# Two attention layers on one core: layer 0's result transposed in 32x32 blocks on VectorE, other shared sums for q, k and v, narrowing copies and normalisations moved

## The chip, the cores and the metric

The kernel runs on one core of one Trainium2 chip. The metric is the device time of the whole kernel in microseconds (us), the median of several runs. Before the change it is 3349.99 us (three runs, 3349.24 to 3350.64).

## What is computed

There are 4096 nodes with 512 features and a 0/1 adjacency matrix. Layer 0 is a graph attention with 4 heads of 128, layer 1 a masked attention with 8 heads of 64. Both are added to their input and normalised over the features.

```python
# layer 0
support = (x @ weight).reshape(N, 4, 128).transpose(1, 0, 2)
logits = f1[:, None, :] + f2[:, :, None]      # f1, f2: support times weight_u, weight_v
w = where(logits >= 0, logits, 0.2 * logits)
attn = softmax(where(w * adj != 0, w * adj, -1e30)) * mask
x = layernorm(x + attn @ support + bias + x @ proj_w + proj_b)
# layer 1
q, k, v = (einsum('nd,hdk->hnk', x, W) for W in (Wqs, Wks, Wvs))
scores = q @ k.T * 64 ** -0.5 + 0.01 * eye - 1e16 * (1 - max(adj, eye))
x = layernorm(x + einsum('hqm,hmk,hko->qo', softmax(scores), v, Wo))
```

## The kernel before

The work is float32 on TensorE throughout, in three stages after a short start that ends at 216 us in the profile.

**Layer 0** (216 to 1136 us) goes over 4 quarters w of 1024 rows each, in each over 4 heads h (a quarter and head is a pass) and in each pass over 32 steps j, one for each 128 columns. In a step ScalarE makes the signs of the logits (`signs`, L625, two steps at once), VectorE masks them (`front`, L636, two steps at once) and makes the weights p (L641), and TensorE multiplies p with the values (L1076, 8 products, 16 records). The p tiles have four buffers, the z tiles of signs two. VectorE is written three steps ahead of TensorE (`LA = 3`). No scheduler reorders anything: each engine executes its instructions in the order in which the Python program issues them. `beside_unit(w, h, j)` issues, beside step u = 32 h + j of a quarter, the work for the next quarter, and `Later` runs a function a given number of steps later.

That work turns the adjacency into the form in which it is needed. A narrowing copy (`narrow`, L589) is a DMA on GpSimd's queue that reads a block of 1024 x 512 values in float32 and writes it as bf16 to DRAM; before it VectorE writes a token and GpSimd copies it, so that the copy starts when VectorE has come to that point. `turn_in0` (L595) transposes the block by DMA, on SP's queue, into one of two stage tiles. `shrink` (L601) is four ScalarE instructions that narrow it to fp8, and `keep` (L606) stores it for layer 1. A quarter has 8 such blocks c. SP's queue also carries, at the sixth step of each pass, the next pass's factors and values (3 MB, L616 and L987).

After the last head of a quarter `finish` divides (L1026), adds the projection by an accumulating DMA (L1040), and `close` takes the statistics of each of the quarter's eight row tiles (L511 and L513 on VectorE, L515 to L520 on GpSimd); `normalise` scales (L1049) and stores the tile to `x1_d`. `turn` then transposes the tile with four TensorE instructions (L1057), `turned` copies the result out of PSUM (L1062) and stores it to `x1T_d`, from which layer 1 reads it. In the last quarter the closing work runs on beside the first set of layer 1.

**q, k and v** (1137 to 1428 us) are made for 4 pairs of 512-row groups. For each pair there are three sets, k, q and v, and each is a product of 2x2 blocks done with seven block products instead of eight (`gemm`); `order` gives their order, `of_weights` and `of_features` the sums that they take as operands, and the plain ones take blocks as they are. A block product is 8 records of 0.43 us. Three of the seven accumulate in the PSUM tile of an earlier one. ScalarE, VectorE and GpSimd take the products out, combine and store them. The weights (`load_w`) are loaded with four DMAs each; wk in layer 0, wq and wv at the start of the stage. `beside` holds what is issued after a product. PSUM tiles come from `ps`, three buffers in the banks that layer 0's accumulators had, and from `xp`, two banks in which layer 0's transposes land.

**Attention of layer 1** (1428 to 3335 us): scores (L1127), exponential (L1341), mask (L1344), product with v (L1389), row sums on GpSimd and by accumulating DMAs (L1364, L1374), the output projection (L1453), and the closing normalisation.

## Time and profile before

| what | value |
|---|---|
| median of three runs | 3349.99 us |
| the profiled execution's own time | 3350.18 us |
| its span, first to last instruction | 3348.4 us |
| mean granted TensorE clock | 0.998 |
| TensorE busy | 3325.1 us (99%) |
| VectorE, ScalarE, GpSimd busy | 70%, 59%, 66% |
| TensorE transposes L1057 | 128 records, 19.2 us busy |
| ScalarE copies of them L1062 | 32, 18.5 us busy |
| ScalarE waiting for a transposed block (L601) | 9.5 us in 3 waits |

A row of the groups names line, engine, operation, output and inputs with their shapes, count, busy time and the mean of one in ns. A row of the waits says who waited for whom, for how long in total, how often and how long at most. A row of the timeline gives start and length in us, and in brackets the idle time before it and what ended it. TensorE's instructions overlap, so the sum of their lengths is more than the time that they take from one another; their starts tell that time.

### The profile page before, as it was taken

To read this page: it belongs to the slowest core of one execution; us is meant where nothing else is said; L and a number is where in the kernel's file an instruction comes from. 1 tells how busy PE (TensorE), PEld (TensorE's weight loads), DVE (VectorE), ACT (ScalarE), POOL (GpSimd) and SP (SyncE) were. 2 spreads that over 40 slices of the span, in tenths; PEclk is the share of its full clock that TensorE was granted. 3 is DMA by queue.
4 is the path that set the end of the run, shared out by engine and by line. 5 is a ranking of instruction groups with operands and counts; after the bars stand their busy time and mean duration, and the time that the engine had idled before them with its cause. 6 is when DMAs were issued, how large, how long until landed. Compare 5 with 4: busy or idle time off the path is not lost.

```text
span 3348.4 us, 66683 instructions
## 1 busy us (share of the span) xinstructions
PE 3325.1 (99%) x27096; PEld 1953.1 (58%) x27096; DVE 2359.6 (70%) x2894; ACT 1986.6 (59%) x2463; POOL 2218.8 (66%) x1588
## 2 busy tenths in 40 slices
PE   9999999999999999999999999999999999999998
PEld 8899999999999755643333333333333333333332
DVE  6689899898999611167776667676666666667676
ACT  1366977878776421256666656566565656656564
POOL 5631040040020365589999999999999999999996
PEclk9999999999999999999999999999999999999999
DMA  8988869589531443379899998889988889887984
GB/s 181 229 191 163 241 152 200 145 197 186 149 105 64 117 160 114 135 204 211 199 209 220 223 208 187 212 195 245 212 191 211 192 204 255 189 211 187 212 195 112
DMA packets 399054, 620.41 MB, mean 185 GB/s; under 512 B 166672, under 2 KB 247568, under 8 KB 397712
## 3 DMA queue, kind: packets, MB, share of 16 engines
q0 software_dynamic: 97520, 258.77, 42.5%
q1 hardware_dynamic: 299344, 354.26, 34.8%
q8 instruction: 215, 3.52, 0.4%
q10 hardware_dynamic: 1872, 3.02, 0.3%
q14 instruction: 103, 0.84, 0.1%
HBM read 315.87 MB, written 117.64 MB: 129 GB/s over the span
## 4 chain that ended last, share of the span: by engine, by line
PE 96%; POOL 1%; DVE 1%; issue 1%; DMA 1%; ACT 0%; SPq 0%; POOLq 0%; ACTq 0%; DVEq 0%
PE o_ps L1076 27%; PE o_ps L1389 26%; PE s_ps L1127 26%; PE s_ps L1192 5%; PE o_ps L847 4%; PE s_ps L1453 3%; PE s_ps L1185 3%; PE s_ps L1408 1%; PE x_ps L1057 0%; DMA p<-p 0%; DVE p L1521 0%; POOL q_sum L1364 0%; POOL s L700 0%; PE x_ps L1185 0%; DVE prod L818 0%
## 5 line engine op out<-in xcount | busy, mean ns | idle before, releaser
L1364 POOL TENSOR_TENSOR q_sum<-q_sum,p 128x1024 f32<-128x1024 f32 x538 | 1374.9, 2556 | 63.0 <-DMA p<-p 39.2
L1344 DVE TENSOR_TENSOR p<-s_ps,adjT 128x1024 f32<-128x1024 f32 x896 | 1043.8, 1216 | 465.3 <-ACT s_ps L1341 436.5
L1341 ACT ACTIVATE s_ps<-s_ps 128x1024 f32<-128x1024 f32 x1021 | 967.1, 1006 | 594.5 <-PE s_ps L1127 594.3
L1389 PE MATMUL o_ps<-p,v_sb 64*64 64x512 f32 x8192 | 943.6, 590 | 0.0
L1127 PE MATMUL s_ps<-q_sb,k_sb 64*64 64x512 f32 x8192 | 942.8, 589 | 0.2 <-DVE p L1344 0.2
L1076 PE MATMUL o_ps<-sup_t,p 128*128 128x129 f32 x8192 | 919.4, 275 | 1.2 <-DVE p L641 1.2
L1076 PEld LDWEIGHTS o_ps<-sup_t,p 128*128 128x128 f32 x8192 | 917.0, 192 | 1.6 <-DVE p L641 1.4
L641 DVE SCALAR_TENSOR_TENSOR p<-fr_t,dj,az 128x1024 f32<-128x1024 f32 x512 | 652.8, 1284 | 80.4 <-PE o_ps L1076 53.1
L1389 PEld LDWEIGHTS o_ps<-p,v_sb 64*64 64x64 f32 x8192 | 310.3, 133 | 570.6 <-issue 560.3
L1127 PEld LDWEIGHTS s_ps<-q_sb,k_sb 64*64 64x64 f32 x8192 | 312.8, 133 | 566.1 <-issue 456.1
L625 ACT ACTIVATE z<-fr_t,f 128x1024 fp8e4<-128x1024 f32 x512 | 558.0, 1144 | 119.4 <-DVE az L636 119.0
L1374 POOL DMA_DIRECT2D p<-p x412 | 437.2, 1297 | 10.2 <-PE o_ps L1389 8.5
L1040 POOL DMA_DIRECT2D agg<-base_d x32 | 28.7, 1206 | 516.0 <-ACT agg L1026 515.8
L1344 DVE TENSOR_TENSOR p<-s_ps,md 128x1024 f32<-128x1024 f32 x128 | 150.7, 1217 | 68.3 <-ACT s_ps L1341 63.6
L588 POOL COPY seen<-token 128x1 f32<-128x1 f32 x24 | 13.6, 565 | 252.9 <-DVE token L586 252.9
L636 DVE TENSOR_TENSOR az<-adjT,z 128x512 int32<-128x512 int32 x256 | 175.5, 686 | 2.1 <-ACT z L625 1.4
L1199 ACT ACTIVATE sb<-s_ps 128x1024 f32<-128x1024 f32 x35 | 35.8, 1024 | 192.6 <-PE s_ps L1192 129.8
L601 ACT ACTIVATE adjT<-stage 128x1024 fp8e4<-128x1024 bf16 x128 | 130.6, 1051 | 9.5 <-DMA stage<-adj_d 9.5
L1214 POOL TENSOR_TENSOR sb<-sb,sb 128x1024 f32<-128x1024 f32 x36 | 84.9, 2373 | 72.2 <-ACT sb L1199 72.2
L1238 DVE COPY k_sb<-s_ps 128x1024 f32<-128x1024 f32 x12 | 14.7, 1225 | 141.0 <-PE s_ps L1192 91.3
L1453 PE MATMUL s_ps<-wo_sb,on 128*128 128x512 f32 x240 | 110.8, 604 | 0.0
L1423 ACT ACTIVATE r<-r_h 32x256 f32<-32x256 f32 x248 | 102.3, 412 | 2.9
(179 smaller groups left out, 2139.4 us busy)
## 6 DMA issues: line engine op xcount, KB each, us to landing
p<-p POOLq DMA_DIRECT2D x412, 512.0 KB, 9.0
k_sb<-k_d SPq DMA_DIRECT2D x128, 512.0 KB
v_sb<-v_d SPq DMA_DIRECT2D x128, 512.0 KB
adj_d<-in_adj_dram POOLq DMA_DIRECT2D x32, 1024.0 KB, 10.9
sup_t<-sup_d SPq DMA_DIRECT2D x120, 258.0 KB
fr_t<-fr_d SPq DMA_DIRECT2D x16, 1024.0 KB
adjT_d<-adjT SPq DMA_DIRECT2D x32, 512.0 KB
adjT<-adjT_d SPq DMA_DIRECT2D x32, 512.0 KB
```

What stands on the lines that cost most here:

```text
L625: nc.scalar.activation(z[:, k, :], fr_t[w, h][:, 0, :], AF.Sign, bias=fs[j // GT][:, 0, (j + k) % GT, h:h + 1], saturate=False)
L636: nc.vector.tensor_tensor(az.bitcast(I32), adjT[w, j // CJ][:, j % CJ:j % CJ + 2, :].bitcast(I32), z.bitcast(I32), op=ALU.bitwise_and)
L641: nc.vector.scalar_tensor_tensor(p, fr[:, 1, :], dj[j // GT][:, j % GT, h:h + 1], az_t[w, h, j // 2][:, j % 2, :], op0=ALU.max, op1=ALU.mult)
L1076: nc.tensor.matmul(o[t // BK][:, t % BK, :], p[:, t * P:(t + 1) * P], s, start=(j == 0 and t % BK == 0), stop=(j == NT - 1), skip_group_ch ...
L1127: nc.tensor.matmul(s[c:c + MS, e, :], k[r, a + c:a + c + MS], qt[g, m][r, :], start=True, stop=True)
L1192: nc.tensor.matmul(half, a[:, c, n * P:(n + 1) * P], x[:, c, :], start=not more and c == 0, stop=c == 1, skip_group_check=True)
L1341: nc.scalar.activation(s, s, AF.Exp)
L1344: nc.vector.tensor_tensor(p, s, keep[:, None, :].to_broadcast([P, HP, G]), op=ALU.mult)
L1364: nc.gpsimd.tensor_tensor(q, q, p, op=ALU.add)
L1374: later.at(2, lambda: nc.gpsimd.dma_start(a, b, accum_op=ALU.add))
L1389: nc.tensor.matmul(o[c, n, :], v[r, j % CH, c], p[r, e, :], start=(j == 0), stop=(j == NT - 1))
L1453: nc.tensor.matmul(s, on_t[g][:, m, t * P:(t + 1) * P], wo_sb[:, m, :], start=(m == 0), stop=(m == NP1 - 1))
```

## The change

- The transposes of layer 0's result leave TensorE, with `turn`, `turned` and `x1T_d`. `x1_d` is kept by 512-row groups. `load_x1` reads half a group back in pieces of 32 rows by 128 features, and `turn_x1` transposes each 32x32 block on VectorE, into an order of the features that the weights follow (`load_w` loads 16 pieces per weight in that order). The first two groups are read and turned in the last quarter of layer 0, from step 72 on one transpose in three steps; the others in the k, q and v sets of the pair before.
- The seven products take other sums: sums are built on sums, and the results share one partial sum, u2. Feature sums of later pairs move from GpSimd to VectorE. The first product of the first set is of plain blocks and lands in `xp`. wv is loaded after the first set. The scaling of q moves from wq into the exponential.
- The narrowing copies of quarters 1 to 3: for quarter 1 one in 5 steps from step 16; for quarters 2 and 3 three at the end of the quarter before the usual one (steps 113, 118, 123), the other five from step 13. Transpositions start at step 50 or 48, one in 8 steps, and wait for a VectorE memset of two elements of the stage tile; `shrink` follows 8 steps after (14 before) and `keep` 15.
- The statistics of a quarter's tiles follow each other at 5/2 steps, from step 10 on (3/2 from step 12 before), except in the last quarter.

The diff, cut to its core:

```diff
-    order = (2, 3, 4, 5, 1, 6, 7)
...
+    order = (1, 5, 2, 6, 7, 3, 4)
+    of_weights = {5: ((1, 0), (1, 1), ALU.add), 6: (5, (0, 0), ALU.subtract),
+                  7: ((0, 0), (1, 0), ALU.subtract), 3: ((0, 1), 6, ALU.subtract)}
+    of_features = {5: ((0, 1), (0, 0), ALU.subtract), 6: ((1, 1), 5, ALU.subtract),
+                   7: ((1, 1), (0, 1), ALU.subtract), 4: ((1, 0), 6, ALU.subtract)}
+    plain_weights = {1: (0, 0), 2: (0, 1), 4: (1, 1), 7: (1, 0)}
+    plain_features = {1: (0, 0), 2: (1, 0), 3: (1, 1)}
...
             stage[w, c] = adjT_p.tile([P, CJ, W], BF16, name="stage", bufs=2)
+            if w:
+                nc.vector.memset(stage[w, c][:, 0, 0:2], 0.0)
             nc.sync.dma_start_transpose(stage[w, c], adj_d[w][c])
...
+        ys, xTs = {}, {}
+
+        def load_w(dst, src, c, a):
+            f = a * P + c * SQ
+            nc.sync.dma_start(dst[a * SQ:(a + 1) * SQ, c],
+                              src[:, f:f + SQ, :].rearrange("h p k -> p h k"))
+
+        def load_x1(g, n, pool=turn_p):
+
+
+
+            if n == 0:
+                xTs[g] = pool.tile([P, KC, G], F32, name="xT1", bufs=2)
+            ys[g, n] = turn_p.tile([P, HG // SQ, P], F32, name="y1_sb", bufs=2)
+            for a in range(NQ):
+                nc.sync.dma_start(
+                    ys[g, n][a * SQ:(a + 1) * SQ],
+                    x1_d[g][n * HG:(n + 1) * HG, a * P:(a + 1) * P].rearrange(
+                        "(b r) f -> r b f", r=SQ))
+
+        def turn_x1(g, n, c):
+            nc.vector.transpose(
+                xTs[g][:, c, n * HG:(n + 1) * HG].rearrange("p (b r) -> p b r", r=SQ),
+                ys[g, n][:, :, c * SQ:(c + 1) * SQ])
...
-                        first, step = (44, 9) if w else (52, 8)
-                        if u == (16 + 8 * c if w else 22 + 7 * c):
+                        first, step = (48, 8) if w else (50, 8)
+                        if u == (13 + 5 * (c - 3) if w else 16 + 5 * c) and c >= min(3, 3 * w):
                             narrow(w + 1, c)
+                        if c < 3 and w + 2 < NW and u == 113 + 5 * c:
+                            narrow(w + 2, c)
                         if u == first + step * c:
                             turn_in0(w + 1, c)
-                        if u == min(first + 20 + step * c, H0 * NT - 1):
+                        if u == first + 15 + step * c:
                             keep(w + 1, c)
                         if w == 0 and u == 98 + 3 * c:
                             keep(0, c)
                         for k in range(CJ):
-                            if u == first + 14 + step * c + 4 * k // 3:
+                            if u == first + 8 + step * c + 4 * k // 3:
                                 shrink(w + 1, c, k)
-                elif u % 4 == 0 and NT <= u < NT + 4 * KC:
-                    load_w(wk, wks, (u - NT) // 4)
-                elif u == NT + 4 * KC + 16:
+                elif NT <= u < NT + KC * NQ:
+                    load_w(wk, wks, (u - NT) // NQ, (u - NT) % NQ)
+                elif u == NT + KC * NQ + CJ:
                     nc.vector.tensor_tensor(wk_low, block(wk, 1, 0), block(wk, 1, 1), op=ALU.add)
-                elif h == H0 - 1 and j in (NT // 2, NT // 2 + CJ):
-                    load_xT((j - NT // 2) // CJ)
+                elif u >= 2 * NT and u % CJ == 0:
+                    k = (u - 2 * NT) // CJ
+                    if k % 3 == 0 and k < 12:
+                        load_x1(k // 6, k // 3 % 2)
+                if w + 1 == NW and u >= 2 * NT + 8 and (u - 2 * NT - 8) % 3 == 0:
+                    k = (u - 2 * NT - 8) // 3
+                    if k < 16:
+                        turn_x1(k // 8, k // 4 % 2, k % 4)
...
-                        later.at(12 + (3 * t // 2 if w + 1 < NW else 2 * t),
+                        later.at(10 + 5 * t // 2 if w + 1 < NW else 12 + 2 * t,
...
-                    nc.sync.dma_start(x1_d[i], y)
-                later.at(6, normalise)
-                later.at(8 if w + 1 < NW else 11, lambda: turn(y, i))
...
+                    nc.sync.dma_start(x1_d[i // GT][i % GT * P:(i % GT + 1) * P, :], y)
+                later.at(5 if w + 1 < NW else 6, normalise)
...
-            for dst, src in ((wq, wqs), (wv, wvs)):
+            def load_all(dst, src):
                 for c in range(KC):
-                    load_w(dst, src, c)
+                    for a in range(NQ):
+                        load_w(dst, src, c, a)
+
+            load_all(wq, wqs)
...
+            wk_s, wq_s = [spare()], [spare() for _ in range(2)]
+            wk_s = {5: wk_low, 6: wk_s[0][:, 0], 3: wk_s[0][:, 1], 7: block(wk, 1, 0)}
+            wq_s = {5: wq_s[0][:, 0], 6: wq_s[0][:, 1], 3: wq_s[1][:, 0], 7: block(wq, 1, 0)}
+            wv_s = {i: sp.tile([P, 2, D // 2], F32, name=f"wv_s{i}", bufs=1) for i in (5, 6, 3)}
+            wv_s[7] = block(wv, 1, 0)
...
+                a, c = (sums[k] if isinstance(k, int) else block(w, *k) for k in (a, c))
...
+                a, c = (x_s[k] if isinstance(k, int) else features(pair, *k) for k in (a, c))
...
-                sb = {i: sp.tile([P, 2 * G], F32, name=f"sb{i}", bufs=1) for i in (2, 3, 1)}
+                u2, p5 = (sp.tile([P, 2 * G], F32, name=n, bufs=2) for n in ("u2", "p5"))
...
                 for i in order:
-                    if i in (2, 3) or i == 6:
+                    if i == (7 if last else 1 if kind == "k" and pair == 0 else 0):
+                        t[i] = [xp.tile([P, GT, P], F32, name="x_ps").rearrange(
+                            "p t r -> p (t r)") for _ in range(2)]
+                    elif i in (1, 5, 6, 7):
                         t[i] = new()
-                    elif i == 1:
-                        t[i] = [xp.tile([P, GT, P], F32, name="x_ps").rearrange(
-                            "p t r -> p (t r)") for _ in range(2)] if last else new()
                     else:
-                        t[i] = t[{4: 2, 5: 3, 7: 1}[i]]
-                    if i == 7 and last:
+                        t[i] = t[{2: 1, 3: 5, 4: 7}[i]]
+                    if i == 4 and last:
                         for n in range(3):
                             first[n] = score(0, 0, n)
-                            nc.scalar.activation(first[n], first[n], AF.Exp)
-                    product(i, t[i], more=i in (4, 5, 7))
-                    if i in sb:
-                        copy(sb[i], t[i])
-                    if i == 3:
-                        pool(sb[3], sb[3], sb[2], ALU.subtract)
-                    elif i == 4:
+                            nc.scalar.activation(first[n], first[n], AF.Exp, scale=float(KD) ** -0.5)
+                    product(i, t[i], more=i in (2, 3, 4))
+                    if i == 1:
+                        copy(u2, t[i])
+                    elif i == 5:
+                        copy(p5, t[i])
+                    elif i == 2:
+                        copy(out["11"], t[i])
+                        store("11")
+                    elif i == 6:
+                        add(u2, t[i])
+                    elif i == 7:
+                        add(out["22"], t[i])
+                        pool(out["22"], out["22"], p5, ALU.add)
+                        later.at(1, lambda: store("22"))
+                    elif i == 3:
+                        add(out["12"], t[i])
+                        store("12")
+                    elif last:
                         copy(out["21"], t[i])
+                        pool(out["21"], out["21"], u2, ALU.add)
+                        store("21", nc.gpsimd)
+                    else:
+                        add(out["21"], t[i])
                         store("21")
...
                         fn()
                     later.step()
...
+                more = pair + 1 < NG // 2
+                halves = [(2 * pair + 2 + n // 2, n % 2) for n in range(4)] if more else []
+
+                def bring(n):
+                    load_x1(*halves[n], turn_p if pair % 2 else sp)
+
+                def turn(n):
+                    for c in range(KC):
+                        turn_x1(*halves[n], c)
+
                 beside = {}
...
+                    combine_features(nc.vector, 0, 5)
+                    for n, i in ((1, 6), (5, 7), (2, 3)):
+                        beside.setdefault(n, []).append(
+                            lambda i=i: combine_weights(nc.vector, wk, wk_s, i))
+                    for n, i in ((1, 6), (5, 7), (2, 4)):
+                        beside.setdefault(n, []).append(
+                            lambda i=i: combine_features(nc.vector, 0, i))
+                    for i, n in ((5, 7), (6, 7), (7, 3), (3, 4)):
                         beside.setdefault(n, []).append(
                             lambda i=i: combine_weights(nc.gpsimd, wq, wq_s, i))
+                if more:
+                    for k, n in ((5, 0), (7, 1)):
+                        beside.setdefault(k, []).append(lambda n=n: bring(n))
+                if pair == 0:
+                    beside.setdefault(4, []).append(lambda: load_all(wv, wvs))
                 gemm(wk, wk_s, "k", pair, beside)
                 beside = {}
                 if pair == 0:
...
+                    for i, n in ((5, 5), (6, 2), (7, 6), (3, 7)):
+                        beside.setdefault(n, []).append(
                             lambda i=i: combine_weights(nc.gpsimd, wv, wv_s, i))
-                if pair == NG // 2 - 1:
+                if more:
+                    for k, fn, n in ((1, turn, 0), (5, turn, 1), (5, bring, 2), (6, bring, 3),
+                                     (4, turn, 2)):
+                        beside.setdefault(k, []).append(lambda fn=fn, n=n: fn(n))
+                else:
...
-                if pair + 1 < NG // 2:
-                    for i in of_features:
-                        beside.setdefault(i, []).append(
-                            lambda i=i: combine_features(nc.gpsimd, pair + 1, i))
+                if more:
+                    beside[1] = [lambda: turn(3)]
+                    for i, n in ((5, 5), (6, 6), (7, 7), (4, 4)):
+                        beside.setdefault(n, []).append(
+                            lambda i=i: combine_features(nc.vector, pair + 1, i))
...
-                    nc.scalar.activation(s, s, AF.Exp)
+                    nc.scalar.activation(s, s, AF.Exp, scale=float(KD) ** -0.5)
```

## The prediction, made before the changed kernel was run

> **What bounds the kernel now.** I read first the page's busy times, then TensorE's waits, then TensorE in order of time at the places that the change touches, then what VectorE and the queues do beside it.
>
> ```profile
> PE 3325.1 (99%) x27096; PEld 1953.1 (58%) x27096; DVE 2359.6 (70%) x2894; ACT 1986.6 (59%) x2463; POOL 2218.8 (66%) x1588
> ```
>
> TensorE is busy 3325.1 of 3348.4 us, and its own list of waits is nearly empty. Of its longer rows these three touch the change:
>
> ```profile
> PE o_ps L1076 <- DVE p L641: 1.2, 1, 1.2
> PE s_ps L1192 <- ACT agg L1026: 1.1, 1, 1.1
> PE s_ps L1192 <- POOL adjT L1156: 0.7, 1, 0.7
> ```
>
> So from 216 us on the span is a sum of matmul work: time can be won by taking work off TensorE or by removing the last two waits, and by nothing else; it is lost wherever another engine makes TensorE wait. TensorE in order of time, at a normalisation and at the layer boundary (start, duration, count):
>
> ```profile
> 475.79 0.60 PE L1057 MATMUL x_ps<-ident,agg 128*128 128x128 f32 x4
> 476.23 3.74 PE L1076 MATMUL o_ps<-sup_t,p 128*128 128x129 f32 x32
> ...
> 1134.78 1.61 PE L1076 MATMUL o_ps<-sup_t,p 128*128 128x129 f32 x13
> 1137.50 3.70 PE L1192 MATMUL s_ps<-xT,wk_low 128*128 128x512 f32 x8 [1.10 <-ACT agg L1026]
> ```
>
> Four transposes show 0.60 us, but the next matmul starts 0.44 us after they do. The last product of layer 0 ends at 1136.39 and q, k, v begin 1.10 us later.
>
> What can make TensorE wait in layer 0 is VectorE's chain (timeline, one cycle of two steps) and the blocks of adjacency that DMA transposes (timeline of the SP queue and of ScalarE):
>
> ```profile
> 444.98 0.68 DVE L636 TENSOR_TENSOR az<-adjT,z 128x512 int32<-128x512 int32 x1
> 445.77 2.48 DVE L641 SCALAR_TENSOR_TENSOR p<-fr_t,dj,az 128x1024 f32<-128x1024 f32 x2
> 448.17 0.68 DVE L636 TENSOR_TENSOR az<-adjT,z 128x512 int32<-128x512 int32 x1
> ```
> ```profile
> 563.00 11.92 SPq L595 DMA_TRANSPOSE stage<-adj_d  x1
> ...
> 587.29 2.00 ACT L601 ACTIVATE adjT<-stage 128x1024 fp8e4<-128x1024 bf16 x2 [4.07 <-DMA stage<-adj_d]
> ```
>
> VectorE needs 448.17 - 444.98 = 3.19 us for two steps. TensorE needs 32 records: the chain has 1888 records in 210.84 us, 0.1117 each, so 3.57 us. VectorE has 0.19 us a step to spare. The transposed block issued at 563.00 was usable only at 587.29, 24.3 us later, with a narrowing copy in flight (that copy's row: 8.2/10.9/25.0 us to landing, minimum, median, maximum).
>
> **What the Trainium skill says.** "TensorE: Matmul & The Clock Gate", Part 4: PE-mode transpose, gives about 275 ns for a transpose in a kernel, mostly access latency. The trace agrees on the duration (273 ns mean, L1057), but in the stream one costs 0.109 us, so I price by spacing. "VectorE: DVE Perf Modes", The three transpose paths, says that VectorE transposes only 32x32 blocks, each in place in its grid: hence the change's loads in 32-row pieces and its permuted weight loads. Layer 0 of this trace does the same (L741). "DMA: Bandwidth & Descriptors", Issuing engines are not separate DMA queues, says that DMAs of all issuing engines interleave on the same 16 engines; the 24.3 us above agree.
>
> **The change, part by part.**
>
> *Transposes off TensorE.* Two groups of four and 48 records take 482.02 - 475.79 = 6.23 us; 48 x 0.1117 = 5.36; so a group costs 0.87 / 2 = 0.435 us. 32 groups x 0.435 = **13.9 us** off the path: 24 groups (10.4) in layer 0, 8 (3.5) in q, k, v. ScalarE's 32 copies (L1062, 587 ns, 18.5 us) and 32 SP stores go with them; neither is waited for.
>
> *In their place* 64 VectorE transposes 128x256, 413 ns each (L741). Sixteen fall in the last quarter of layer 0, one in three steps: 0.41 against 3 x 0.19 = 0.57 us to spare, so hidden; if there were no cover, 6.6 us. Each waits for its load; queued behind it on VectorE are the next p tiles, and TensorE behind those. The load is issued at least 8 steps (14 us) earlier, from rows written hundreds of us before, in a stretch where DMA is at 0.15 of its share (1000 to 1100); a similar strided load took 5.9 us at the start. So nothing. The other 48 (19.8 us) lie in q, k, v, where VectorE was busy 14.70 of 100 us (1200 to 1300). The loads are 4 SP issues per half in place of one per tile; weights take 16 issues instead of 4. wq is issued before the boundary and needed 24 us (one set of seven products) after it; 16 issues at the 0.72 us of today's larger ones are 11.6 us. wv is issued a set later and needed 48 us after the boundary. Nothing.
>
> *Shared sums.* Seven products a set before and after, three of them accumulating: TensorE's work is the same. A set's evictions go from 4 ScalarE copies, 3 VectorE and 4 GpSimd passes to 3, 4 and 1; the feature sums go from GpSimd (2.35 us) to VectorE (1.2 to 1.9). Each product lasts 3.44 us (8 x 0.43), the longest eviction 1.23, and a PSUM tile is needed again at the earliest one product later, so no wait appears. The first product now takes plain operands and a PSUM tile that nobody else holds: the 1.1 us wait goes; its next need, the first freed bank, is 3.44 us later, and the divisions that free the banks end at 1137.96, before 1136.4 + 3.4. The q set's first product no longer needs a GpSimd sum: **0.7 us** go. What is late next: the fifth product's feature sum, one 1.2 to 1.9 us VectorE instruction from 1136.7, in time. In the last set one thing turns against it: the second early score takes the tile that the product just before it used. That tile is free 1.23 us plus some 0.2 of signalling after the product; the first score covers 0.91 (2.74 for three). **+0.5 us.** wq's scaling (1.9 us on ScalarE) moves into the exponential's scale: nothing.
>
> *Normalisations.* A tile's statistics hold VectorE 0.82 us (458.89 to 459.71). Before, two tiles in three steps: 4.79 + 1.64 = 6.43 against TensorE's 6.23. After, two in five steps: 7.98 + 1.64 = 9.62 against 8.94, because TensorE no longer pauses: 0.68 lost per pair, 2.7 us over four pairs. VectorE's lead is three p buffers less its own instruction, 5.36 - 1.28 - 0.3 = 3.8 us. It holds, with 1.1 us left; without spreading it would not.
>
> *Narrowing copies and transposed blocks.* Three of eight copies go to the end of the quarter before, where DMA was at 0.14 (635 to 645); in quarters 1 and 2 the rest are issued by step 33 and the first transposition comes at 48, so those no longer meet. But a new two-element memset makes each transposition wait for VectorE, and ScalarE takes the block 8 steps (14.3 us) later in program order instead of 14. Behind the memset on VectorE stand the p tiles, but the buffer it waits for was given up 4 steps earlier: nothing. Behind the held transposition on SP stand stores and the next pass's loads, due many steps later. The price is on ScalarE: a block must land about 14.3 - 1.05 (narrowing to fp8) - 2.3 (two signs) = 11 us after the memset or VectorE waits, and some 4 us of VectorE's lead later, 15 us, or TensorE waits. Alone, a block kept DMA busy 0.60 + 0.14 of ten us (625 to 645), 7 us: in time. In quarter 0 all eight copies run at one per 5 steps (8.9 us) and the last overlap the first transposition (step 50 against 46 and 51). Bounds there: 0, if the queues share evenly and the block takes twice its 7 us; 24.3 - 15 = 9 us, if the old collision returns. No gain is possible, since TensorE has no such wait now. I take **+1.2 us**, nearer to zero because only 3 of 32 blocks were waited for (9.5 us in total).
>
> *Sum*, against the profiled execution's own 3350.18 us (span 3348.4 plus 1.8; 0.2 above the runs' median 3349.99, which I leave): 3350.2 - 13.9 - 1.1 - 0.7 + 0.5 + 1.2 = **3336.2 us**.
>
> **Rivals.**
> (a) *The old collision in quarter 0*: 9 us of stall instead of 1.2, 3344.0. For: the 24.3 us row, and copies closer together than before. Against: a lead on ScalarE and VectorE that hid the same lateness then.
> (b) *VectorE becomes layer 0's bound* and the 10.4 us won there are lost to p tiles: 3336.2 + 10.4 - 1.2 = 3345.4, within 0.2%. For: 9.62 against 8.94 in the normalisations. Against: VectorE waited 53.1 us for TensorE in layer 0 (L641's idle row).
> (c) *Slower*: every transposed block of the three quarters (24) lands late, since all now have 8 steps. The place is ScalarE's narrowing; the point is a landing more than 15 us after the memset. The net gain without stalls is 15.2; 0.2% (6.7 us, about what a measurement of this kernel can tell from no change) slower needs (15.2 + 6.7) / 24 = 0.9 us a block. At 2 us a block: 3350.2 - 15.2 + 48 = 3383. For: an SP issue of a transposition takes 6.5 us in the median and up to 15.9. Against: the uncrowded ones take 3.9 to 4.1 and most now run without a copy.
>
> **How the numbers follow.** Forecast 0.62 (3333.5 to 3340), (a) 0.16 (to 3344), (b) 0.13, (c) 0.09. Low end: no stall and no late score (-1.7) and 1.0 for the spread of runs (3349.24 to 3350.64) and rounding, 3333.5. High end: (a), 3344.0; the two hold about 0.8. Faster is below 3343.3: the forecast, (a), and a little of (b), 0.81; same 0.10; slower 0.09.
>
> **What would show it.** Right: no TensorE transposes; q, k, v starting within 0.1 us of layer 0's last product; layer 0 about 10 us shorter and q, k, v about 5; attention unchanged. Wrong: TensorE rows waiting for p (L641's successor) in layer 0, with ScalarE's narrowing waiting for the transposed block (a, c) or VectorE without waits (b); or TensorE waits inside the sets.

## The result, and the profile after

The changed kernel takes 3332.69 us (median of five runs, 3330.72 to 3333.58). The kernel before, timed beside it, took 3350.07 us (3349.24 to 3351.37). The ratio is 0.9946, with a 95% interval of 0.9932 to 0.9961. The forecast was 3336.2 us, and the result lies 0.8 us below its low end of 3333.5. The direction and the main mechanism were forecast; the gain came out larger than the range allowed.

The profiled execution is the longest of the five, 3333.58 us (span 3331.7). I cut both profiles at four marks of TensorE: the first product of layer 0 (`o_ps<-sup_t,p`), the first product of q, k, v, the first score, and the last tiny matmul at the end.

| stage (us) | before | after | difference | forecast |
|---|---|---|---|---|
| start, to layer 0's first product | 209.23 | 209.12 | -0.1 | 0 |
| layer 0 and the boundary | 928.27 | 916.78 | -11.5 | -10.4 - 1.1 + 1.2 |
| q, k, v to the first score | 290.21 | 285.60 | -4.6 | -3.5 - 0.7 + 0.5 |
| attention | 1907.57 | 1908.53 | +1.0 | 0 |
| tail | 13.12 | 11.67 | -1.45 | 0 |

The busy times of the page after answer to the first fence of the prediction. TensorE has 128 matmuls fewer (27096 to 26968) and is still at 99%; VectorE took on work, GpSimd gave some up:

```profile
PE 3310.5 (99%) x26968; PEld 1938.6 (58%) x26968; DVE 2403.4 (72%) x3005; ACT 1955.9 (59%) x2419; POOL 2106.7 (63%) x1535
```

TensorE's list of waits (us in total, times, longest) begins so after the change:

```profile
PE o_ps L846 <- ACT z L863: 3.0, 1, 3.0
PE o_ps L886 <- POOL ident masks.py:199: 1.4, 1, 1.4
PE o_ps L1087 <- DVE p L640: 1.2, 1, 1.2
PE s_ps L1578 <- DVE all_ok L537: 1.0, 1, 1.0
```

The rows for `ACT agg` (1.1) and `POOL adjT` (0.7) are gone. The `DVE p` row is the same single wait of 1.2 us at layer 0's start that the kernel before has; no further wait for p has come. TensorE in order of time at the layer boundary shows the two effects there:

```profile
1099.77 26.29 PE L1087 MATMUL o_ps<-sup_t,p 128*128 128x129 f32 x234
1125.90 3.60 PE L1208 MATMUL x_ps<-xT,wk 128*128 128x512 f32 x8
1129.33 3.60 PE L1208 MATMUL s_ps<-adjT,wk_low 128*128 128x512 f32 x8
```

The group of layer 0 runs to 1126.06 by its modelled end, and q, k, v start at 1125.90 with no bracket, so with no wait. The next product comes 3.43 us later. In layer 0 the engines that prepare p wait like this (ScalarE's and VectorE's rows of waits):

```profile
ACT adjT L600 <- DMA stage<-adj_d: 17.8, 13, 2.7
```
```profile
DVE p L640 <- PE o_ps L1087: 38.9, 131, 0.3
...
DVE az L635 <- ACT z L624: 0.7, 1, 0.7
```

ScalarE now waits for a transposed block 13 times where it did 3 times, but never longer than 2.7 us (4.1 us before). VectorE lost nothing new by that: its one wait of 0.7 us for ScalarE lies at 238.9 us, and the kernel before has it too, at 239.0. VectorE still waited 38.9 us for TensorE, so TensorE remains the bound.

### The profile page after: what moved, and what is told of

Same layout as the page of the kernel before. It is cut to its first block, busy times and chain, and to the rows that moved or that the text cites. A ratio compares the mean times of both kernels' runs of the same rounds, so it can differ in the third digit from the quotient of the medians.

```text
span 3331.7 us, 66521 instructions
## 1 busy us (share of the span) xinstructions
PE 3310.5 (99%) x26968; PEld 1938.6 (58%) x26968; DVE 2403.4 (72%) x3005; ACT 1955.9 (59%) x2419; POOL 2106.7 (63%) x1535
## 4 chain that ended last, share of the span: by engine, by line
PE 95%; POOL 2%; DMA 1%; DVE 1%; issue 1%; ACT 0%; SPq 0%; POOLq 0%; DVEq 0%
PE o_ps L1087 27%; PE o_ps L1424 26%; PE s_ps L1138 25%; PE s_ps L1208 6%; PE o_ps L846 4%; PE s_ps L1488 3%; PE s_ps L1201 3%; DMA p<-p 1%; PE s_ps L1443 1%; POOL q_sum L1399 0%; DMA y_sb<-in_x_dram 0%; DVE p L1556 0%; POOL s L699 0%; PE x_ps L1201 0%; PE x_ps L1208 0%
## 5 line engine op out<-in xcount | busy, mean ns | idle before, releaser
L640 DVE SCALAR_TENSOR_TENSOR p<-fr_t,dj,az 128x1024 f32<-128x1024 f32 x512 | 650.4, 1284 | 67.1 <-PE o_ps L1087 38.9
L1230 POOL TENSOR_TENSOR k_sb<-k_sb,p 128x1024 f32<-128x1024 f32 x12 | 30.7, 2560 | 192.1 <-DVE k_sb L1236 187.8
L1215 ACT ACTIVATE u<-s_ps 128x1024 f32<-128x1024 f32 x11 | 11.3, 1024 | 173.4 <-PE s_ps L1208 110.1
L1236 DVE TENSOR_TENSOR u<-s_ps,u 128x1024 f32<-128x1024 f32 x12 | 14.7, 1225 | 106.2 <-PE s_ps L1208 76.3
```

Source lines behind the costliest of these rows:

```text
L640: nc.vector.scalar_tensor_tensor(p, fr[:, 1, :], dj[j // GT][:, j % GT, h:h + 1], az_t[w, h, j // 2][:, j % 2, :], op0=ALU.max, op1=ALU.mult)
```

## The experiments

Each kernel was timed in five rounds beside the kernel before, whose medians lay at 3350.7 to 3352.6 us. "Layer 0" and "q, k, v" are the stages of the table above, from each kernel's profile.

| kernel | median us | ratio to before, 95% interval | layer 0 | q, k, v |
|---|---|---|---|---|
| again_changed, the changed kernel | 3334.43 | 0.9956 (0.9943 to 0.9969) | 916.76 | 285.60 |
| e1 transposes back | 3346.66 | 0.9985 (0.9979 to 0.9992) | 927.00 | 289.11 |
| e2 old sums | 3336.22 | 0.9959 (0.9947 to 0.9972) | 918.03 | 286.70 |
| e3 old narrowing | 3369.99 | 1.0067 (1.0049 to 1.0085) | 937.44 | 285.61 |
| e4 no spread | 3339.24 | 0.9967 (0.9955 to 0.9978) | 922.13 | 285.61 |
| e5 fp8 copies after 4 steps | 3413.42 | 1.0187 (1.0173 to 1.0200) | 993.10 | 285.60 |
| e6 old narrowing and pauses | 3374.09 | 1.0057 (1.0038 to 1.0076) | 954.20 | 289.12 |
| e7 before with new narrowing | 3349.59 | 0.9998 (0.9990 to 1.0007) | 928.34 | 290.21 |
| e8 stores back | 3352.61 | 1.0003 (0.9995 to 1.0011) | 949.30 | 289.12 |
| e9 addresses back | 3369.67 | 1.0065 (1.0046 to 1.0085) | 944.83 | 289.12 |
| e10 first product in ps | 3334.64 | 0.9950 (0.9938 to 0.9963) | 918.03 | 285.70 |
| e11 no memset | 3338.21 | 0.9961 (0.9948 to 0.9974) | 918.55 | 285.61 |
| e12 old narrowing, memset | 3341.98 | 0.9967 (0.9955 to 0.9980) | 927.06 | 285.60 |
| e13 fp8 copies after 6 steps | 3336.43 | 0.9951 (0.9937 to 0.9964) | 919.66 | 285.60 |

A stage is read from one profiled run, and where runs scatter that run need not be typical: e3's (3357.9 us) and e11's (3333.6 us) were the shortest of their runs, e8's (3371.0 us) the longest. For kernels whose runs scatter (e3, e6, e9) the ratio differs a little from that of the medians. The first four shared one set of runs of the kernel before, e4 to e7 the next, e8 to e11 the third, e12 and e13 the last. again_changed repeats the changed kernel:

> The changed kernel once more, unchanged. Theory: the profile repeats layer 0 (910.1 us from the first wait to q, k, v) and q, k, v (285.6) to 0.2 us; the spread between runs of some 3 us comes from the attention stage and the end. Rival: layer 0 varies by 1 us or more.

It gave 3334.43 us (3333.13 to 3340.59). Layer 0 and q, k, v repeat to 0.02 us between the two profiles; what differs lies in the start, attention and the tail. The longest run, 3340.59 us, was not the profiled one.

**e1: the transposes.** Four TensorE transposes per row tile are put back; nothing reads them.

```
+                later.at(7 if w + 1 < NW else 11, lambda: turn_again(y))
+            def turn_again(y):
+                p = xp.tile([P, KC, P], F32, name="x_ps")
+                for c in range(KC):
+                    nc.tensor.transpose(p[:, c, :], y[:, c * P:(c + 1) * P], ident)
```

> The changed kernel with four TensorE transposes per row tile put back where they stood (two steps after the normalisation, eleven steps after the statistics in the last quarter); nothing reads their result, and the new path by VectorE stays. Theory (the gain is TensorE's own time): 32 groups x 0.435 us = 13.9 us more than the changed kernel, about 3346.6 us, 10.4 of it in layer 0 and 3.5 in q, k, v. Rival (the gain came from the freed ScalarE copies, stores and the new schedule): less than 7 us more, under 3340.

Measured: +12.2 us in the median over again_changed, +12.8 in the profile's span. Layer 0 grew by 10.2 us for 24 groups and q, k, v by 3.5 for 8, which is 0.43 a group in both. The spacing of the instructions was the right price.

**e2: the sums.** The products, sums and evictions of the kernel before, with the new transposes and schedule. With them come the old place of wv's load and the scaling of q in wq.

> The changed kernel with the sums, the order of the seven products and the evictions of the kernel before; transposes by VectorE, loads and schedule of layer 0 as changed. Theory (TensorE's work is the same, only two waits differ): the waits of 1.1 us at the boundary and 0.7 us at the first q set come back, with some 0.1 us each for filling TensorE again: 2.0 us more than the changed kernel, about 3334.7. Rival (the lighter evictions shorten q, k, v as such): the whole 4.6 us by which that stage became shorter beyond layer 0, less the 3.5 us of transposes, is smaller than 2, so to part them the profile must show waits inside the sets; 4 us or more would speak for it.

Measured: +1.8 us in the median. TensorE's list of waits has both rows again:

```profile
PE s_ps L1206 <- ACT agg L1051: 1.1, 1, 1.1
...
PE s_ps L1206 <- POOL adjT L1170: 0.7, 1, 0.7
```

Layer 0 with the boundary is 1.3 us longer and q, k, v 1.1, so each wait costs 0.2 to 0.4 more than its row. Most of this can be seen in the order of time. The row counts from the modelled end of the last record, but without a wait the next product starts 0.16 us ahead of that end (1125.90 against 1126.06 above); and a product that starts after a wait is followed by the next 3.54 us later, not 3.43.

The two experiments together account for both stages: 10.2 + 1.3 = 11.5 us in layer 0 and 3.5 + 1.1 = 4.6 us in q, k, v. So the moved narrowing copies and normalisations won no time of their own; the experiments below show what they prevent.

**e10: the bank of the first product.** One condition is changed.

```
-                    if i == (7 if last else 1 if kind == "k" and pair == 0 else 0):
+                    if i == (7 if last else 0):
```

> The changed kernel with the first product of the first k set in a bank of layer 0's pool again instead of one that nobody else holds. Theory: the 1.1 us wait of TensorE for ScalarE's last divisions returns at the start of q, k, v, with that row in the list of waits, and nothing else: +1.1 us. Rival (the plain operands alone removed it): no wait, within 0.3 us of the changed kernel.

In this kernel's list of waits the row of the boundary is back, in full:

```profile
PE s_ps L1208 <- ACT agg L1049: 1.1, 1, 1.1
```

Layer 0 is 1.3 us longer than in the changed kernel. Plain operands alone would not have removed this wait; the free bank did. The median, 0.2 us over again_changed's from another set of runs, is too coarse to show 1.1 us.

**e4: the spreading of the normalisations.**

```
-                        later.at(10 + 5 * t // 2 if w + 1 < NW else 12 + 2 * t,
+                        later.at(12 + (3 * t // 2 if w + 1 < NW else 2 * t),
...
-                later.at(5 if w + 1 < NW else 6, normalise)
+                later.at(6, normalise)
```

> The changed kernel with the closings and normalisations of a tile spaced as before (two row tiles in three steps instead of five, normalisation a step later); all else as changed. By the prediction VectorE needs two tiles' statistics in three steps: 4.79 + 1.64 = 6.43 us against 5.36 us of TensorE without its pauses, 1.07 us lost per pair, 4.3 us over the four pairs of a quarter, against a lead of 3.8 us. The prediction's step (without spreading it would not hold): TensorE waits for p of about 0.5 us in each of the first three quarters, 1.5 us in all, +1.5 us. Rival (the lead is larger than reckoned, or regained between the pairs): no row of TensorE waiting for p in the middle of layer 0 and the time of the changed kernel within 0.5 us; VectorE's idle time there merely shrinks.

The row of TensorE's waits for p in this kernel:

```profile
PE o_ps L1087 <- DVE p L640: 5.0, 7, 1.2
```

One of the seven is the 1.2 us of every kernel; 3.8 us are new, and layer 0 is 5.4 us longer. The step holds in kind (without spreading, VectorE's lead is used up). I had reckoned 1.5 us in all, so the lead was overrun by more than the 0.5 us a quarter of my sum. The 1.6 us of layer 0 beyond the six waits are again some 0.3 us for each.

**e13 and e5: how late a block may be.** ScalarE takes a block 6 or 4 steps after its transposition instead of 8. e5 has this edit, e13 has a 6 in the same place:

```
-                            if u == first + 8 + step * c + 4 * k // 3:
+                            if u == first + 4 + step * c + 4 * k // 3:
```

> The changed kernel with ScalarE taking a transposed block 6 steps (10.7 us) after the transposition instead of 8. By the prediction's reckoning VectorE waits for blocks that land later than 7.4 us after the memset and TensorE for those later than 11.4 us. The changed kernel's own longest wait of ScalarE for a block was 2.7 us at 8 steps; at 6 steps it would be 6.3 us, at most 2 us more than VectorE's lead. Theory: TensorE waits at a few blocks, under 5 us in all, 3333 to 3340 us. Rival (as with 4 steps, where TensorE's waits came to 55 us, the lead is used up at every block): 20 us or more over the changed kernel.

> The changed kernel with ScalarE taking a transposed block 4 steps (7.15 us) after the transposition was issued instead of 8 (14.3 us). By the prediction's reckoning a block must then land 7.15 - 1.05 - 2.3 = 3.8 us after the memset or VectorE waits, and within about 7.8 us or TensorE waits. The changed kernel's first block was usable after 9.0 us. Theory: VectorE waits for ScalarE at nearly each of the 24 blocks, TensorE for p at the slower ones, about 1 us each, +5 to +30 us, all of it in layer 0; a small result would say that the blocks land sooner than the waits of the changed kernel let one see. Rival (the landing time is not what decides; the queues' order does): within 1 us of the changed kernel.

At 6 steps a single TensorE wait of 2.2 us is new; it follows a ScalarE wait of 5.0 us, so 2.8 us were covered there, while a ScalarE wait of 6.1 us, the longest, passed without any. The prediction's lead of some 4 us lies between the two. At 4 steps these are the rows of ScalarE and of TensorE:

```profile
ACT adjT L600 <- DMA stage<-adj_d: 115.2, 22, 9.8
```
```profile
PE o_ps L1087 <- DVE p L640: 55.3, 33, 3.5
```

Layer 0 grew by 76.3 us, far more than I expected (5 to 30): I had counted 1 us at the slower blocks, but nearly every block was late and the lead did not recover between them. Some 54 us of it are new waits in the row above; six stretches of 3.4 us at half clock (last section) make some 10 us more. So the price of a late block is small up to a point and steep beyond it, and the change stands two to four steps from that point.

**e3: the old narrowing schedule.** Copies, transpositions, fp8 copies and stores at the steps of before, without the memset; all else as changed.

```
-            if w:
-                nc.vector.memset(stage[w, c][:, 0, 0:2], 0.0)
...
-                        first, step = (48, 8) if w else (50, 8)
-                        if u == (13 + 5 * (c - 3) if w else 16 + 5 * c) and c >= min(3, 3 * w):
+                        first, step = (44, 9) if w else (52, 8)
+                        if u == (16 + 8 * c if w else 22 + 7 * c):
...
```

> The changed kernel with the narrowing copies, transpositions, fp8 copies and stores of the adjacency at the steps of the kernel before, and without the memset ahead of the transposition. Theory (the moves hide nothing that was late before): the same time within 1 us; ScalarE waits some 10 us in 3 or so waits as before, TensorE not at all. Rival (with TensorE no longer pausing, VectorE's smaller reserve no longer covers a block that lands 24 us after its issue): TensorE waits in layer 0, 4 to 9 us more.

The theory was wrong, and the rival right that TensorE would wait, but far too small: 3370 us, 36 us over the changed kernel and slower than the kernel before, though that kernel uses the same steps without a wait. (The rival's reason, the missing pauses, falls with e6 below.) In quarter 1 the SP queue begins with the transpositions while the third narrowing copy, issued by GpSimd at 495.92, is still in flight; that copy landed at 513.5:

```profile
508.82 57.74 SPq L592 DMA_TRANSPOSE stage<-adj_d  x3
```
```profile
495.92 0.87 POOL L586 DMA_DIRECT2D adj_d<-in_adj_dram  x1
509.42 0.75 POOL L586 DMA_DIRECT2D adj_d<-in_adj_dram  x1
```
```profile
543.98 1.06 ACT L598 ACTIVATE adjT<-stage 128x1024 fp8e4<-128x1024 bf16 x1 [12.78 <-DMA stage<-adj_d]
```

The three issues hold the queue for 57.74 us, and the first block is usable after 543.98 - 508.82 = 35.2 us. In the kernel before, the same three issues took 38.30 us from 510.06; the third copy had landed 0.4 us before that, and the fourth had been issued 0.5 us before:

```profile
510.06 38.30 SPq L595 DMA_TRANSPOSE stage<-adj_d  x3
```
```profile
494.84 0.77 POOL L589 DMA_DIRECT2D adj_d<-in_adj_dram  x1
509.52 0.75 POOL L589 DMA_DIRECT2D adj_d<-in_adj_dram  x1
```

**e7: is the schedule worth anything by itself?** The kernel before with the new steps and the memset only.

> The kernel before with one part of the change alone: narrowing copies a quarter ahead, the new steps of transposition, fp8 copies and stores, and the memset; transposes stay on TensorE, sums as before. In the kernel before TensorE had no wait for these blocks, so this part alone removes nothing: within 0.3 us of the kernel before, 3350 to 3351 us. Rival (the part gains by itself, or loses by blocks landing after the 8 steps): a difference of more than 1 us, seen as a shorter or longer layer 0.

No difference (0.9998, 0.9990 to 1.0007), with layer 0 at 928.34 us against 928.27. So the part gains nothing alone, and in the changed kernel its lack costs 20 us and more (layer 0 of e3).

**e6, e8, e9, e12: why the old schedule broke.** Three causes could be named: TensorE no longer pauses, DRAM buffers lie elsewhere because the turned result's buffers are gone, or SP's queue lacks 32 stores of 256 KB and so runs ahead. e6 is e3 with the old pauses and normalisations. e8 adds to e6 stores of the result, unturned, at the old step. e9 has the DRAM layout of e8 but only tiny stores. Their lines for this, e8 first, then e9:

```
+                nc.sync.dma_start(x1T_d[i // GT][:, :, i % GT * P:(i % GT + 1) * P],
+                                  y.rearrange("p (c f) -> p c f", c=KC))
...
+                if i % GT == 0:
+                    nc.sync.dma_start(x1T_d[i // GT][0:1, 0, 0:P], y[0:1, 0:P])
```

> The changed kernel with the old schedule of narrowing copies, transpositions, fp8 copies and stores (as in the experiment that gave 3370 us), and also the old spacing of the normalisations and four unused TensorE transposes per row tile at the old steps, so that TensorE pauses where it did before and layer 0's engines do what they did before, except that there are no copies and stores of the turned result. Theory A (the pauses of TensorE and the slack they give VectorE and ScalarE made the old schedule hold): layer 0 as in the kernel before, about 928 us, and the whole 13.9 us over the changed kernel, 3347 to 3348. Theory B (what holds or breaks is how the copies and transpositions meet in the DMA engines, and that is set by where the buffers lie and the queue's other traffic, not by TensorE's pauses): blocks again usable 25 to 35 us after issue and 3355 to 3385 us.

> The kernel of the experiment with the old narrowing schedule, old normalisation spacing and unused TensorE transposes (3374 us), and besides the 32 stores of 256 KB that the kernel before made of the turned result, at their old step on the SP queue (they store the result a second time, unturned; nobody reads it). Its blocks of quarters 2 and 3 lie at the same DRAM addresses as before but for the first two of each. Theory (the stores held SP's queue and the DMA engines so that copies and transpositions met less): copies land in 12 us in the median again in quarters 1 and 2, no TensorE wait in the middle of layer 0, 3347 to 3350 us. Rival 1 (the addresses decide): the same, and the next kernel too. Rival 2 (neither decides): copies at 22 to 26 us, 3355 to 3380 us.

> The same, but with only 8 stores of 512 bytes instead of the 32 of 256 KB, so that the DRAM addresses are those of the kernel just before this one and the traffic is that of the slow kernel. Theory (the stores' traffic decides): slow, 3355 to 3380 us, copies at 22 to 26 us. Rival 1 (the addresses decide): 3347 to 3350 us, copies at 12 us. Rival 2 (neither): slow, together with the kernel just before.

e6 gave 3374 us (two of its eight runs 3355), so the missing pauses are not the cause. e9 gave 3370 us (six runs, 3363.0 to 3385.0), so the addresses are not. e8 gave 3352.6 us; 11 of its 13 runs lie between 3347.0 and 3356.2, the other two at 3364 and 3371. That is above the 3347 to 3350 us of its theory, but 17 us below e9, which differs from it in the stores' traffic alone. So this traffic mostly restores the old behaviour, but not safely. The profile of e8 is of its longest run and shows what goes wrong there, not a typical run. e12 then holds SP back in another way: it is e3 with the memset alone.

```
+            if w:
+                nc.vector.memset(stage[w, c][:, 0, 0:2], 0.0)
```

> The kernel of the experiment with the old narrowing schedule (3370 us), with the memset ahead of each transposition of the three quarters put back and nothing else. In the profiles so far a quarter stayed free of waits where the first transposition was issued 15.3 us or more after the third copy (three of four such quarters), and stalled where it was issued 8.7 to 12.9 us after it (six of six), with the third copy still in flight. The memset holds the first transposition of quarters 1 and 2 to VectorE's step 44, about 78 us after the quarter's start and some 20 us after the third copy. Theory (SP running ahead is what broke the old schedule): copies at about 12 us in the median, no TensorE wait for p in quarters 1 and 2, within 3 us of the changed kernel, 3332 to 3338 us. Rival (copies issued during the transpositions are enough to break it, and only moving them helps): copies at over 20 us and 3350 us or above.

The same lines in quarter 1 of e12 (SP's queue, then GpSimd's issues):

```profile
513.66 35.08 SPq L594 DMA_TRANSPOSE stage<-adj_d  x3
```
```profile
494.32 0.87 POOL L586 DMA_DIRECT2D adj_d<-in_adj_dram  x1
507.82 0.75 POOL L586 DMA_DIRECT2D adj_d<-in_adj_dram  x1
```

A tiny VectorE instruction ahead of each transposition of the three quarters, with no copy moved, takes the median from 3370 to 3342 us. It holds every one of them, so e12 does not tell whether the start of the first or the spacing of the others counts. The quarters of these profiles side by side (landing is the median of a quarter's eight copies; the wait is TensorE's for p):

| kernel, quarter | first transposition after the third copy's issue, us | copies' landing, us | wait, us |
|---|---|---|---|
| before, 1 and 2 | 15.2, 15.6 | 12.1, 11.7 | 0, 0 |
| e3, 1 and 2 | 12.9, 12.6 | 22.5, 22.5 | 5.3, 5.7 |
| e6, 1 and 2 | 8.5, 8.8 | 23.9, 26.1 | 6.8, 11.9 |
| e9, 1 and 2 | 10.3, 9.0 | 25.2, 17.0 | 13.9, 0 |
| e8, 1 and 2 | 18.2, 17.1 | 13.3, 25.8 | 2.8, 14.1 |
| e12, 1 and 2 | 19.3, 19.7 | 11.2, 12.7 | 2.4, 4.5 |

Up to 12.9 us, all six quarters have slow copies (17 us and more in the median); from 15.2 us on, five of six have fast ones. This is no rule of the distance alone. In quarter 0 of before, e3, e6, e8 and e9 the first transposition comes only 0.5 to 1.2 us after the third copy's issue, and yet the copies land in 8.5 to 9.1 us; what differs there stays open. My count of waits ahead of e12 was too clean, as the table shows: e9's second quarter had no wait, and e8's first had one of 2.8 us. e12 is 7.6 us over again_changed, outside the 3332 to 3338 us of the theory. What is left there is one block a quarter whose transposition meets the last two copies; ScalarE waits 9.9 us for it in quarter 1 and 12.0 us in quarter 2. In the changed kernel, where the copies are moved, those waits are gone. Why one quarter of e8 stalled with a late transposition stays open.

**e11: the memset in the new schedule.** The two lines of e12 taken out of the changed kernel.

> The changed kernel without the two-element memset that holds each transposition of the three quarters until VectorE comes to its step. The prediction counted the memset at nothing as a cost. Theory: without it SP runs ahead to the transpositions as soon as a buffer is free, up to some steps early, and they meet the copies again in quarter 0, where copies are still in flight, and there only: ScalarE waits a little more, TensorE at most 3 us, 3331 to 3336 us. Rival (the memset is what keeps copies and transpositions apart in all quarters): copies at over 15 us in the median, TensorE waits of 10 us or more, 3345 us or above.

The theory held in kind: only in quarter 0 does a block come very late (ScalarE waits 9.8 us), and there the copies land in 15.4 us in the median, in quarters 1 and 2 in 12.0. TensorE's waits for p are 2.6 us in two pieces, 1.4 of them new, and layer 0 is 1.8 us longer. But this is the profile of its shortest run; the median, 3338.2 us, is above the 3331 to 3336 us of the theory and 3.8 us over again_changed, with ratios whose intervals overlap. So with the moved steps the memset is worth some 2 to 4 us, not clear of the noise; with the old steps it was worth 28 us of the median (e3 against e12).

## Why the prediction was too high

**Right, as written.** Transposes off TensorE: 13.9 us forecast; 13.7 by e1's two stages (10.2 + 3.5). The boundary wait, 1.1 us, and the q set's wait, 0.7 us, went: e2 brings both back, e10 the first alone. The 16 VectorE transposes in the last quarter are hidden: TensorE has no wait there. Loads, weights and evictions at nothing: no row of TensorE names any of them. Spreading keeps VectorE ahead (e4). ScalarE's margin for a block: 8 steps leave no TensorE wait, 6 one of 2.2 us, 4 more than 50 us. The 11 us after which VectorE waits come out too: at 6 steps the same sum gives 7.4 us, and there the first block of quarter 0, usable after 8.9 us, made VectorE wait 1.4 us.

**Failed: the +1.2 us for a block beside the narrowing copies in quarter 0.** Nothing was lost. ScalarE in that stretch, after the transposition issued at 294.52, when copies were still in flight:

```profile
303.52 1.06 ACT L600 ACTIVATE adjT<-stage 128x1024 fp8e4<-128x1024 bf16 x1 [2.65 <-DMA stage<-adj_d]
...
316.66 1.06 ACT L600 ACTIVATE adjT<-stage 128x1024 fp8e4<-128x1024 bf16 x1 [0.92 <-DMA stage<-adj_d]
```

The block was usable after 9.0 us, against the 24.3 us of the old collision and the 15 us at which TensorE would wait. Both bounds were right; the value between them should have been the lower one, and the memset is part of the reason (e11 shows 9.8 us of waiting there without it). I had counted it as a cost of nothing and missed that it is a benefit: it keeps SP from running ahead. "Most now run without a copy" was the right argument against rival (c), but only the schedule and the memset make it so: e3, which lacks just these two, ends slower than the kernel before, and so do e6 and e9.

**Failed: the +0.5 us for the second early score.** No time was lost. The three early scores are 24 records in 2.81 us without a gap, before and after:

```profile
1427.71 2.81 PE L1127 MATMUL s_ps<-q_sb,k_sb 64*64 64x512 f32 x24
```
```profile
1411.50 2.81 PE L1138 MATMUL s_ps<-q_sb,k_sb 64*64 64x512 f32 x24
```

The wait I charged to the change, a weight load that waits for VectorE to empty a tile, exists in both kernels with the same numbers. It stands before the third score, not the second (16 of the 24 loads are ahead of it, and a score has eight):

```profile
1429.15 0.15 PEld L1127 LDWEIGHTS s_ps<-q_sb,k_sb 64*64 64x64 f32 x4 [0.38 <-DVE v_sb L1245]
```
```profile
1412.94 0.15 PEld L1138 LDWEIGHTS s_ps<-q_sb,k_sb 64*64 64x64 f32 x4 [0.38 <-DVE v_sb L1236]
```

I worked out a cost from the code and did not look whether the trace of before already had it. Against the usual spacing of 0.43 us the load is 0.1 us late in both, and the matmuls that it feeds start 0.43 us after those before them, so TensorE lost none of it.

**Missing: what a wait costs beyond its row.** q, k, v gained 4.6 us where 4.2 had been added up. e2 shows 1.1 us for a row of 0.7. A removed wait gives back some 0.2 to 0.4 us more than its row (e2, e10).

**Too narrow: the spread of runs.** I allowed 1.0 us below. Attention (+1.0), the tail (-1.45) and the start (-0.1) add to -0.6 us between the two profiles. This is chance as far as can be told: over all profiles here attention lies between 1907.3 and 1908.9 us and the tail between 11.5 and 13.5, whatever the kernel. And the profiled execution is the longest of five that spread over 2.9 us, 0.9 above their median. Together, 1.2 + 0.5 + 0.4 + 0.6 + 0.9 = 3.6 us, and 3336.2 - 3332.7 = 3.5 is explained to rounding. The low end had room for the first two alone and 1.0 for the rest, which came to 1.9. The repeat's 3334.43 us lies inside the range.

## What to carry to other kernels

Price a removed instruction by the spacing it causes in the stream, and before charging a new wait to a change, look for the same row in the trace of before. A queue that nothing holds runs ahead of its program: when stores or loads on it go, what stands behind them moves forward and can meet other transfers, so a schedule that held by such cover is safer held by something explicit. A part of a change that is worth nothing on the old kernel can be what makes the rest pay.

## What the runs showed of the hardware

A long wait of TensorE costs more than itself. In e6 TensorE waited 7.3 us up to 830.31; the windows around it (length, PE busy and records, granted clock, DMA share, GB/s):

```profile
810.00:820.00 10.00, 10.00 (x92) 1.00 1.27 68
820.00:830.00 10.00, 3.05 (x28) 0.76 1.27 227
830.00:840.00 10.00, 9.69 (x64) 0.73 1.64 260
840.00:850.00 10.00, 10.00 (x92) 1.00 0.82 172
```

In the ten microseconds after the wait the granted clock (the share of full speed that TensorE was given) was 0.73 in the mean, and 64 records ran instead of 92. The 28 records at 0.109 us are 3.0 us, of which 0.3 is the end of the wait itself. In finer windows the clock is at 0.50 from 825.22 to 835.46 and then full again; 18 records run in a window at half clock, 32 in the next:

```profile
832.05:835.46 3.41, 3.41 (x18) 0.50 1.04 339
835.46:838.87 3.41, 3.41 (x32) 1.00 3.01 276
```

The Trainium skill ("TensorE: Matmul & The Clock Gate", Part 1: What's actually happening) says that after an idle window of some 3.4 us the clock falls to half, until a busy window of that length has passed, and that these windows run freely, whatever the kernel does. The trace agrees on the windows: the 10.24 us of half clock are three of 3.41 us, the first idle, the second half busy (TensorE resumes at 830.31), the third busy. But a window need not be wholly idle. In e12 a wait of 2.4 us, up to 595.75, left TensorE busy for 1.39 us of one window, and the next was at half clock:

```profile
591.95:595.37 3.42, 1.39 (x13) 1.00 0.96 284
595.37:598.78 3.41, 3.03 (x14) 0.50 0.00 0
```

After e5's wait of 2.4 us up to 326.18 the clock stayed at 1.00; counted back in windows of 3.413 us from the half clock that this trace shows at 362.93, that wait lay across a border (325.38). I counted all windows so from 209 to 1190 us, in the profiles whose half clocks fix the borders. Each of the 19 full-clock windows in which TensorE was busy for at most 0.41 of the time was followed by half clock, and none of those with 0.44 or more. So two waits of the same length can cost differently, by some 1.7 us (half of 3.41), by where they fall.

DMA engines can be occupied and move little. In the first window of e6 above, the packets' times add up to a share of 1.27 of the DMA engines (a packet counts whole in the window where it starts, so this can pass 1), but only 68 GB/s were moved, with two narrowing copies and a transposed block in flight together; in the next window, at the same share, 227. The skill ("DMA: Bandwidth & Descriptors", Issuing engines are not separate DMA queues) says that DMAs of all issuing engines run on the same 16 DMA engines and interleave, which fits; how strongly a copy and a transposition slow each other, from 12 to over 30 us for a copy (e6, e8 and e9 in quarters 1 and 2), only these runs show.
